# First graph-attention layer: masks straight from the transposes, two sets of mask tiles, a part of chunk 0 made in the loop

## The chip, the cores and the metric

The kernel runs on one core of a Trainium2 chip. The metric is the device time of one execution in microseconds (us); lower is better. The core has TensorE (PE), VectorE (DVE), ScalarE (ACT) and GpSimd (POOL). SyncE (SP) computes nothing here; it issues most of the transfers, one after the other, from its own queue, and a transfer that has to wait holds up those behind it.

## The reference, cut to what matters

There are N = 4096 nodes with 256 features and an adjacency matrix of 4096 x 4096 int32. Layer 0 is a graph attention and an FFN of 30 steps; layer 1 has two graph attentions and a routed FFN of six experts. All three graph attentions use the same adjacency:

```
h  = einsum('nf,hfd->hnd', layernorm(x), W)         # 4 heads of 64
f1 = h . a1 ; f2 = h . a2                           # per node and head
e  = leaky_relu(f1[:, :, None] + f2[:, None, :], 0.2)
e  = where(adj > 0, e, -9e15)
out = elu(softmax(e) @ h)
```

## The kernel before, in words

**The attention without an exponential per pair.** exp of a leaky ReLU is one of two products, exp(f1)exp(f2) or its version with slope 0.2; which one is told by the sign of f1 + f2. So per node j the preparation writes two scaled copies of h (tile `vals`, in two f16 parts), and the loop only makes, for every pair, a byte that says which copy counts: `st` where the sign says "above" and the edge exists, `below` where the edge exists and the sign says otherwise. PE multiplies `vals` by these byte tiles (FP8, 0x38 is 1.0).

**The order.** `attention` is called for g0 (layer 0), g1 and g2 (layer 1). Each call has a preparation over 8 groups of 512 nodes (`columns`, `products`, `upper`, `lower`; L259 to L383) and then a loop over 128 units: 4 chunks of 1024 target nodes, 4 heads, 8 blocks q of 4 x 128 source nodes. In the loop a unit has
- four steps (`step_of`, L445): `st` <- sign(f1 + f2), on ACT (L459), or for the fourth step of some units on DVE (L457: two units of five in chunks 0 to 2 of g0, else four of five). Steps are written one unit ahead (LEAD = 1); the tile `st` has 4 buffers.
- two DVE instructions, L585 (`st` and mask) and L591 (mask xor `st`, into `below`, 3 buffers).
- 64 matmuls of the unit before (L535).
- at times an instruction of the closing of the head before (L466 to L497, L631, L632).

**The masks.** A mask tile `m` holds one group g of 1024 source nodes for one chunk: 1 MB as bytes, made of four pieces. A piece starts as 256 rows x 1024 columns of adj (1 MB int32, `rows_a`, 3 buffers, loaded at L203), is turned to bytes by one DVE instruction (L211, `rows_p`) and transposed by a DMA (L217). In g0 the 16 pieces of chunk 0 are made in the preparation, two after each group (`first_masks`, L222), straight into the four buffers of `m`, and each full tile is stored to `edges` in DRAM (L230). The pieces of chunk c + 1 are made in the loop of chunk c, by a generator (`make`, L502) that takes one unit for load, conversion and transpose into the tile `turned`, and the next unit for the store of these 256 KB to `edges` (L513). From chunk 1 on the loop reads its masks back from `edges` (`load_mask`, L191, called at L600). Layers g1 and g2 load every mask from `edges`.

**What sets the order.** Tile pools are opened and closed as a stack: a pool opened after the preparation's pools are closed lies in the memory these had, and the first instruction that writes there waits for the last one that used it. The pool `work` of the loop (L439), with `st` and `below`, is such a pool, and so is `end` (closings) in g0; in g1 and g2 `end` is opened before the preparation (L182). DVE and ACT run the loop in the written order (`manual_schedule`, L553). Everything else is ordered by a planner with its own estimates of costs: it may put an instruction that is ready ahead of one that stands earlier in the code, in the loop's surroundings too.

**Rows.** x and later rows come through the pool `stream` (4 buffers of 512 KB, L61, loaded at L96 on SP). At the end of g0's loop the first groups of x1d, the layer's result, are asked for (L607); the FFN takes these four groups at L705, measures them (L682, L684), and computes their rates on ACT and POOL (L690 to L694), for which it needs the constants `eps` (L661, POOL).

Of the kernel before, what the change touches and what calls it, by code (L numbers as in the profile page):

```python
# [11 lines left out]
F32 = mybir.dt.float32  # L12
# [34 lines left out]
def gnn_ffn_kernel(ctx: ExitStack, tc: tile.TileContext, a: dict, out: bass.AP):  # L47
# [13 lines left out]
    stream = ctx.enter_context(tc.tile_pool(name="stream", bufs=4))  # L61
# [26 lines left out]
    ahead = {}  # L88


    def rows_in():
        return stream.tile([P, G * C], F32, name="rows")

    def load_ahead(src, g, view=rows_of):
        t = rows_in().rearrange("p (r c) -> p r c", c=C)
        nc.sync.dma_start(t, view(src, g))  # L96
        ahead[g] = t
# [67 lines left out]
    def attention(tag, src, norm, w, others, chunks, first, ends, following):  # L165
# [7 lines left out]
        with ExitStack() as scope:  # L173
# [5 lines left out]
            mask = scope.enter_context(tc.tile_pool(name=f"{tag}_mask", bufs=4))  # L179
            fpool = scope.enter_context(tc.tile_pool(name=f"{tag}_f", bufs=2))  # L180

            end = None if first else scope.enter_context(tc.tile_pool(name=f"{tag}_end", bufs=1))  # L182
            masks, f1b = {}, {}
# [7 lines left out]
            def load_mask(c, g):  # L191

                m = masks[c, g] = mask.tile([P, 4, 8, TR], F8, name="m")
                nc.sync.dma_start(m, edges[c, g])

            arow, prow = {}, {}

            def load_piece(c, n):

                g, part = n // 4, n % 4  # L200
                i0 = c * CM * P + part * TR
                arow[n] = pieces.tile([P, 2, 8 * P], I32, name="rows_a", bufs=3)
                nc.sync.dma_start(  # L203
                    arow[n],
                    adj[i0 : i0 + TR, g * 8 * P : (g + 1) * 8 * P].rearrange("(p s) n -> p s n", s=2),
                )

            def to_bytes(n):

                prow[n] = pieces.tile([P, 8 * P, 2], I8, name="rows_p", bufs=2)  # L210
                nc.vector.tensor_scalar(  # L211
                    prow[n].rearrange("p n s -> p s n"), arow.pop(n), 0, ONE8, op0=OP.is_gt, op1=OP.mult
                )

            def turn(dst, n):

                nc.sync.dma_start_transpose(  # L217
                    dst.rearrange("p j n -> p (j n)").bitcast(BF16).rearrange("p (j n) -> p j n", j=8),
                    prow.pop(n).rearrange("p n s -> p (n s)").bitcast(BF16),
                )  # L220

            def first_masks(n):  # L222

                g, part = n // 4, n % 4
                if part == 0:
                    masks[0, g] = mask.tile([P, 4, 8, TR], F8, name="m")
                to_bytes(n)
                turn(masks[0, g][:, part], n)
                if part == 3:
                    nc.sync.dma_start(edges[0, g], masks[0, g])  # L230

            with ExitStack() as ps:
# [19 lines left out]
                def load(g):  # L252
                    if g in ahead:
                        rows[g] = ahead.pop(g)
                    else:
                        load_ahead(src, g)
                        rows[g] = ahead.pop(g)
# [126 lines left out]

                if first:
                    load_piece(0, 0)
                load(0)
                load(1)
                if first:
                    for n in (1, 2):  # L390
                        load_piece(0, n)
                if not first:
                    load_mask(0, 0)
                late = [functools.partial(make, prep, small_ps, get(prep)) for get, make in others]
                for g in range(NG + 2):
# [14 lines left out]
                    if first:  # L410
                        for n in range(2 * g, min(2 * g + 2, 16)):
                            first_masks(n)
                            if n + 3 < 16:
                                load_piece(0, n + 3)
# [21 lines left out]

            if first:
                end = scope.enter_context(tc.tile_pool(name=f"{tag}_end", bufs=1))
# [4 lines left out]
            steps, accs = {}, {}  # L443

            def step_of(at, s):  # L445
# [5 lines left out]
                if s == 0:  # L451
                    steps[at] = work.tile([P, 4, JU, TR], I8, name="st", bufs=4)
# [47 lines left out]
            todo = []  # L500

            def make(c):  # L502

                load_piece(c, 0)
                load_piece(c, 1)
                for n in range(16):
                    if n + 2 < 16:
                        load_piece(c, n + 2)
                    to_bytes(n)
                    t = pieces.tile([P, 8, TR], F8, name="turned", bufs=3)  # L510
                    turn(t, n)
                    yield
                    nc.sync.dma_start(edges[c, n // 4, :, n % 4], t)  # L513
                    yield

# [34 lines left out]
            closing, making = None, None  # L552
            with tc.manual_schedule(engines={mybir.EngineType.DVE, mybir.EngineType.Activation}):  # L553
# [3 lines left out]
                for at in range(len(units) + LAG):  # L557
# [5 lines left out]
                    if at < len(units):  # L563
                        c, h, q = units[at]
                        if q == 0 and h == 0 and first and c + 1 < len(chunks):
                            making = make(c + 1)
# [26 lines left out]
                    if b >= 0:  # L593
# [5 lines left out]
                        if bh == H - 1 and bq % 2 == 1 and bc + 1 < len(chunks):  # L599
# [3 lines left out]
                    if making is not None:  # L603
                        next(making, None)
                    if at == len(units) - (4 if first else 2):
                        for g in range(3 if first else 2):
# [37 lines left out]
    attention("g0", x, True, w0, [make, *makers], [8, 8, 8, 8], True, to_rows(x1d, x), [x1d])  # L644
# [9 lines left out]
    with ExitStack() as scope:  # L654
# [16 lines left out]
        def load(g):  # L671
            if g not in ahead:
                load_ahead(x1d, g)
# [31 lines left out]
        for g in range(4):  # L705
            load(g)
# [652 lines left out]
```

## Time and profile before

| what | us |
|---|---|
| time, median of 3 runs (3040.38 to 3043.03) | 3040.51 |
| the profiled execution: its time | 3040.38 |
| its span on the profile | 3038.7 |
| PE / DVE / ACT / POOL busy, of the span | 2810.8 / 2713.6 / 2423.7 / 1160.5 |
| g0: first L585 of the loop; L585 of unit 96 (first of chunk 3) | 108.76; 488.32 |
| end of g0's loop on DVE (last L591) | 605.2 |
| g1: first L585 of the loop | 1663.24 |
| g2: first L585 of the loop | 2206.39 |

How to read it: the windows view gives the busy time of each engine in a stretch, with the number of instructions in brackets. A timeline line gives start and duration in us, engine, line of the code, operation, output <- input tiles, shape and count; what stands in square brackets is the idle time of the engine just before and what ended it. Instructions of one engine overlap a little, so the distance from start to start is a few hundredths of a us shorter than the duration. "SPq" is SP's queue. "st<-f1b,nf" and "vals<-v" name tiles without their buffer numbers.

### The profile page before, as it was taken

What the parts mean: (1) busy time and instruction counts of PE and PEld (TensorE: products, weight loads), DVE (VectorE), ACT (ScalarE), POOL (GpSimd) and SP (SyncE); (2) the same over time, 40 slices, a digit from 0 to 9 for tenths busy, and PEclk for the clock granted to TensorE, in tenths of its full rate; (3) what the DMA queues carried; (4) which work ended last, traced back from release to release, by engine and by line L of the source; (5) the groups of instructions that cost most, each with busy time, mean ns of one, the idle gap of its engine ahead of it and who ended that gap; (6) DMA issues with size and microseconds to landing.
All of it is one profiled execution on the core that took longest, in us unless ns stands there. A gap on an engine that the chain in (4) does not pass through costs nothing. (4 is left out here: it accounts for less than half of the span.)

```text
span 3038.7 us, 80983 instructions
## 1 busy us (share of the span) xinstructions
PE 2810.8 (93%) x33327; PEld 2549.8 (84%) x33327; DVE 2713.6 (89%) x5529; ACT 2423.7 (80%) x3011; POOL 1160.5 (38%) x1052
## 2 busy tenths in 40 slices
PE   6799999969999999999998999999899999975994
PEld 5699999958888888888876999999699999964883
DVE  8799999989999999999997899999789999975445
ACT  4799999888888888888866999999699999951220
POOL 2000000079999999999992000000300000022762
PEclk9899999979999999999998999999999999987997
DMA  9989995143333333333343032120302232141225
GB/s 307 275 246 291 270 266 147 29 132 67 70 67 67 70 67 69 69 67 70 67 98 113 20 102 71 55 85 20 110 23 92 66 95 87 37 146 56 96 93 200
DMA packets 491339, 332.55 MB, mean 109 GB/s; under 512 B 417342, under 2 KB 446171, under 8 KB 484827
## 3 DMA queue, kind: packets, MB, share of 16 engines
q1 hardware_dynamic: 476722, 301.81, 37.3%
q0 software_dynamic: 7104, 19.41, 2.0%
q10 hardware_dynamic: 7144, 6.16, 0.7%
q8 instruction: 263, 4.31, 0.6%
q14 instruction: 106, 0.86, 0.1%
HBM read 195.58 MB, written 52.04 MB: 81 GB/s over the span
## 5 line engine op out<-in xcount | busy, mean ns | idle before, releaser
L535 PE MATMUL acc<-vals,st 128*128 128x130 f16 x12288 | 1431.9, 219 | 59.8 <-DVE st L585 32.0
L535 PE MATMUL acc<-vals,below 128*128 128x130 f16 x12288 | 1431.3, 221 | 2.2 <-DVE below L591 2.2
L459 ACT ACTIVATE st<-f1b,nf 128x1024 int8<-128x1024 f32 x1265 | 1331.0, 1141 | 10.0 <-DMA fd<-rt 6.1
L535 PEld LDWEIGHTS <-st 128*128 128x128 fp8e4 x12288 | 1208.8, 98 | 33.4 <-issue 33.4
L535 PEld LDWEIGHTS <-below 128*128 128x128 fp8e4 x12288 | 1177.5, 96 | 36.4 <-issue 33.4
L869 PE MATMUL po<-wT,zT 128*128 128x256 f32 x1920 | 576.1, 382 | 7.1 <-ACT zT L852 7.1
L872 PE MATMUL po<-w,zT 128*128 128x256 f16 x3840 | 577.9, 273 | 0.4 <-DMA zT<-z 0.4
L833 POOL TENSOR_TENSOR th<-th,y 128x1024 f32<-128x1024 f32 x240 | 567.4, 2364 | 27.3 <-ACT th L832 5.0
L872 PEld LDWEIGHTS <-zT 128*128 128x128 f16 x3840 | 376.3, 98 | 161.9 <-DMA zT<-z 1.5
L591 DVE TENSOR_TENSOR below<-m,st 128x1024 int32<-128x1024 int32 x384 | 470.0, 1224 | 32.7 <-DVE st L585 0.9
L585 DVE TENSOR_TENSOR st<-st,m 128x1024 int32<-128x1024 int32 x384 | 467.7, 1218 | 13.7 <-ACT st L459 13.7
L809 DVE SCALAR_TENSOR_TENSOR y<-po,z_rs,bias 128x256 f32<-128x256 f32 x928 | 384.4, 477 | 2.0 <-PE tp L802 0.7
L845 DVE BATCH_NORM_STATS2 z_st<-z 128x6 f32<-128x256 f32 x960 | 335.7, 413 | 0.0
L869 PEld LDWEIGHTS po<-wT,zT 128*128 128x128 f32 x1920 | 291.1, 192 | 17.1 <-ACT zT L852 8.7
L821 ACT ACTIVATE z<-th 128x1024 f32<-128x1024 f32 x240 | 251.1, 1046 | 8.6 <-POOL th L833 8.3
L832 ACT ACTIVATE th<-y 128x1024 f32<-128x1024 f32 x240 | 249.9, 1041 | 0.1
L856 POOL TENSOR_TENSOR z_rs<-z_rs,mhalf 128x4 f32<-128x4 f32 x240 | 244.7, 1019 | 0.0
L852 ACT COPY zT<-tp 128x512 f32<-128x512 f32 x240 | 140.2, 584 | 110.4 <-PE tp L802 110.3
L457 DVE TENSOR_SCALAR st<-f1b,nf 128x1024 int8<-128x1024 f32 x271 | 201.2, 743 | 5.4 <-DMA fd<-rt 2.7
L661 POOL MEMSET eps<- 128x1 f32 x1 | 0.1, 98 | 520.1 <-DVE u L487 520.1
L1028 POOL IOTA along_i<- 128x37 int32 (+1 forms) x2 | 2.4, 1212 | 501.5 <-DMA ew<-in_L_ffn_expert_w_dram 501.5
L435 POOL MEMSET hs<- 128x4 f32 x3 | 0.3, 101 | 495.0 <-DVE u L487 495.0
(233 smaller groups left out, 3021.5 us busy)
## 6 DMA issues: line engine op xcount, KB each, us to landing
rows_a<-in_adj_dram SPq DMA_DIRECT2D x64, 1024.0 KB
m<-edges SPq DMA_DIRECT2D x44, 1024.0 KB
f1b<-fd SPq DMA_DIRECT2D x48, 512.0 KB
edges<-turned SPq DMA_DIRECT2D x48, 256.0 KB
y<-yd SPq DMA_DIRECT2D x16, 512.0 KB
rows<-x1d SPq DMA_DIRECT2D x12, 512.0 KB
ew<-in_L_ffn_expert_w_dram SPq DMA_DIRECT2D x18, 256.0 KB
rows<-in_x_dram SPq DMA_DIRECT2D x8, 512.0 KB
```

The costliest lines, as they stand in the source:

```text
L459: nc.scalar.activation(out, f1, AF.Sign, bias=f2, scale=-1.0)
L535: nc.tensor.matmul(acc[:, i, cols], masked[part][:, at_i // TR, s, rows], v[:, cols], start=(j == 0 and part == 0), stop=(j == NT - 1 and ...
L585: nc.vector.tensor_tensor(above, above, whole, OP.bitwise_and)
L591: nc.vector.tensor_tensor(below, whole, above, OP.bitwise_xor)
L809: nc.vector.scalar_tensor_tensor(y[:, g * G + r, :], po[:, r, :], rstd[:, r : r + 1], last if end else bias, op0=OP.mult, op1=OP.add,)
L821: nc.scalar.activation(z, th.pop(u), AF.Silu, scale=0.01)
L832: nc.scalar.activation(th[at], y[:, g * G : (g + 1) * G, :], AF.Tanh, scale=0.01)
L833: ins = nc.gpsimd.tensor_tensor(th[at], th[at], y[:, g * G : (g + 1) * G, :], OP.add)
L845: nc.vector.bn_stats(st[:, r, :], z[:, r, :])
L856: nc.gpsimd.tensor_tensor(rs[u], rs[u], mhalf, OP.pow)
L869: nc.tensor.matmul(po[:, r, :], src[:, r * P : (r + 1) * P], wT, start=True, stop=False)
L872: nc.tensor.matmul(po[:, r, :], src16[:, part * G + r, :], w16[:, other, :], start=False, stop=(part == 1 and other == 1),)
```

## The change

The change does these things:
- In g0 a second set of four mask tiles (`mask1`) is opened after the preparation. Chunks 0 and 2 use the first set, chunks 1 and 3 the second. Every transpose writes straight into a mask tile; `turned`, the stores of 256 KB and the reload of chunks 1 to 3 are gone. A full tile is stored once, 1 MB, two pieces after it is full.
- 12 of the 16 pieces of chunk 0 are made in the preparation (1 or 2 after each group). Pieces 12 to 15 are made in the units 0 to 3 of the loop, the 16 of chunk 1 in the units 4 to 31; later chunks have one piece in two units.
- The int32 piece `adj` has 2 buffers instead of 3, in a pool that is closed after g0 and whose place `stream` then takes. The load of piece n + 2 is issued after the conversion and transpose of piece n. In g0 the x rows come through a tile `t` of the preparation, 3 buffers, and the first group of x is issued ahead of the first piece.
- `st` gets a pool of its own, opened ahead of the preparation, in all three layers. `end` is opened after the preparation in all three.
- The FFN's first four loads of x1d are issued from POOL instead of from SP at the end of g0's loop.

```diff
-    stream = ctx.enter_context(tc.tile_pool(name="stream", bufs=4))
+    stream = []
-    def load_ahead(src, g, view=rows_of):
-        t = rows_in().rearrange("p (r c) -> p r c", c=C)
-        nc.sync.dma_start(t, view(src, g))
+    def load_ahead(src, g, view=rows_of, queue=nc.sync):
+        t = stream[-1].tile([P, G, C], F32, name="rows")
+        queue.dma_start(t, view(src, g))
...
-            mask = scope.enter_context(tc.tile_pool(name=f"{tag}_mask", bufs=4))
+            mask = [scope.enter_context(tc.tile_pool(name=f"{tag}_mask", bufs=4))]
-            end = None if first else scope.enter_context(tc.tile_pool(name=f"{tag}_end", bufs=1))
+            spool = scope.enter_context(tc.tile_pool(name=f"{tag}_steps", bufs=4))
...
+            PREP = 12
+            PER = 4 * (NT // 8)
+            def load_piece(n):
+                c, g, part = n // PER, n % PER // 4, n % 4
+                i0 = c * CM * P + part * TR
-                arow[n] = pieces.tile([P, 2, 8 * P], I32, name="rows_a", bufs=3)
+                arow[n] = stream[-1].tile([P, 2, 8 * P], I32, name="adj")
                 nc.sync.dma_start(arow[n], ...)
+            def make_piece(n):
+                if n >= len(chunks) * PER:
+                    return
+                c, g, part = n // PER, n % PER // 4, n % 4
+                if part == 0:
+                    masks[c, g] = mask[c % 2].tile([P, 4, 8, TR], F8, name="m")
+                pair = pieces.tile([P, 8 * P, 2], I8, name="pair")
+                nc.vector.tensor_scalar(pair..., arow.pop(n), 0, ONE8, op0=OP.is_gt, op1=OP.mult)
+                nc.sync.dma_start_transpose(masks[c, g][:, part]..., pair...)
+                if n + 2 < len(chunks) * PER:
+                    load_piece(n + 2)
+                if part == 1 and n > 4:
+                    store_mask(n // 4 - 1)
+            def store_mask(n):
+                c, g = n // (PER // 4), n % (PER // 4)
+                nc.sync.dma_start(edges[c, g], masks[c, g])
...
+                    elif first:
+                        rows[g] = work.tile([P, G, C], F32, name="t", bufs=3)
+                        nc.sync.dma_start(rows[g], rows_of(src, g))
...
+                load(0)
                 if first:
-                    load_piece(0, 0)
-                load(0)
+                    load_piece(0)
                 load(1)
                 if first:
-                    for n in (1, 2):
-                        load_piece(0, n)
+                    load_piece(1)
...
                     if first:
-                        for n in range(2 * g, min(2 * g + 2, 16)):
-                            first_masks(n)
-                            if n + 3 < 16:
-                                load_piece(0, n + 3)
+                        for n in range(PREP * g // 8, min(PREP * (g + 1) // 8, PREP)):
+                            make_piece(n)
...
+            end = scope.enter_context(tc.tile_pool(name=f"{tag}_end", bufs=1))
             if first:
-                end = scope.enter_context(tc.tile_pool(name=f"{tag}_end", bufs=1))
+                mask.append(scope.enter_context(tc.tile_pool(name=f"{tag}_mask1", bufs=4)))
...
-                    steps[at] = work.tile([P, 4, JU, TR], I8, name="st", bufs=4)
+                    steps[at] = spool.tile([P, 4, JU, TR], I8, name="st")
...
-                        if bh == H - 1 and bq % 2 == 1 and bc + 1 < len(chunks):
+                        if not first and bh == H - 1 and bq % 2 == 1 and bc + 1 < len(chunks):
                             load_mask(bc + 1, bq // 2)
...
-                    if making is not None:
-                        next(making, None)
-                    if at == len(units) - (4 if first else 2):
-                        for g in range(3 if first else 2):
+                    if first:
+                        u = at % (H * NJ)
+                        if at < H * NJ:
+                            due = PREP + u + 1 if u < PER - PREP else PER + (u - 3) * PER // 28
+                        else:
+                            due = PER * (at // (H * NJ) + 1) + (u + 1) // 2
+                        while made < due:
+                            make_piece(made)
+                            made += 1
+                        if at == len(units) - 30:
+                            store_mask(len(chunks) * PER // 4 - 1)
+                    if not first and at == len(units) - 2:
+                        for g in range(2):
                             load_ahead(*following[:1], g, *following[1:])
...
-    attention("g0", x, True, w0, [make, *makers], [8, 8, 8, 8], True, to_rows(x1d, x), [x1d])
+    with tc.tile_pool(name="adj", bufs=2) as adjacency:
+        stream.append(adjacency)
+        attention("g0", x, True, w0, [make, *makers], [8, 8, 8, 8], True, to_rows(x1d, x), [])
+    stream.append(ctx.enter_context(tc.tile_pool(name="stream", bufs=4)))
...
         for g in range(4):
-            load(g)
+            load(g, nc.gpsimd)
```

## The prediction

> **What bounds the kernel now.** I read the windows first, one for the preparation of layer g0 and one for each chunk of its loop.
>
> ```profile
> core 0: us, PE busy (x) PEld busy (x) DVE busy (x) ACT busy (x) POOL busy (x), PEclk, DMA share, GB/s
> 108.00:234.00 126.00, 117.42 (x1958) 116.70 (x1959) 117.06 (x119) 126.00 (x127) 0.00 (x0) 0.96 0.95 271
> 234.00:361.00 127.00, 122.48 (x2088) 121.98 (x2086) 122.66 (x130) 126.30 (x128) 0.00 (x0) 0.99 1.02 276
> 361.00:488.00 127.00, 121.15 (x2065) 120.65 (x2063) 123.22 (x131) 126.82 (x129) 0.00 (x0) 0.99 1.03 267
> 488.00:604.00 116.00, 113.31 (x1958) 112.82 (x1956) 110.13 (x124) 106.88 (x109) 0.00 (x0) 1.00 0.15 41
> ```
>
> ```profile
> 12.00:103.00 91.00, 65.16 (x275) 50.52 (x273) 81.38 (x169) 40.75 (x67) 25.14 (x40) 0.90 1.00 301
> ```
>
> In chunks 0 to 2 ScalarE (ACT) has no free time, VectorE (DVE) has 9, 4 and 4 us, and the DMA engines are busy throughout. In chunk 3, which makes no masks, TensorE (PE) is nearest to full. In the preparation DVE is the busiest engine (81 of 91 us); ACT is half idle. DVE's conversions (L211) waited for nothing there: the lines view gives their 64 instructions 0.1 us of idle time.
>
> Next, the timeline where the preparation meets the loop:
>
> ```profile
> 98.13 2.44 DVE L376 SCALAR_TENSOR_TENSOR vals<-vals,v 128x1040 f16<-128x1040 f16 x2
> 99.20 0.23 ACT L340 COPY rt<-sp 32x128 f32<-32x128 f32 x1
> 100.49 2.36 DVE L211 TENSOR_SCALAR rows_p<-rows_a 128x2048 int8<-128x2048 int32 x2
> 103.50 0.64 SPq L341 DMA_DIRECT2D fd<-rt  x1
> 105.50 7.39 ACT L459 ACTIVATE st<-f1b,nf 128x1024 int8<-128x1024 f32 x7 [6.07 <-DMA fd<-rt]
> 105.52 1.42 DVE L457 TENSOR_SCALAR st<-f1b,nf 128x1024 int8<-128x1024 f32 x2 [2.67 <-DMA fd<-rt]
> 108.76 1.23 DVE L585 TENSOR_TENSOR st<-st,m 128x1024 int32<-128x1024 int32 x1 [1.83 <-ACT st L459]
> 110.20 0.37 PE L535 MATMUL acc<-vals,st 128*128 128x130 f16 x2 [14.09 <-DVE st L585]
> ```
>
> The first step tiles (L459, L457) wait for a DMA that reads rt, a tile of the preparation. They need no data from it; they wait because they lie in memory that the preparation gives back. Then DVE waits for ACT's three steps, and PE starts 14 us after its last work. Layer g1 has the same joint (g2 too: last L376 over at 2203.1, first L585 at 2206.39):
>
> ```profile
> 1657.51 2.44 DVE L376 SCALAR_TENSOR_TENSOR vals<-vals,v 128x1040 f16<-128x1040 f16 x2
> 1659.98 12.58 ACT L459 ACTIVATE st<-f1b,nf 128x1024 int8<-128x1024 f32 x12 [1.31 <-DVE vals L376]
> 1663.24 1.22 DVE L585 TENSOR_TENSOR st<-st,m 128x1024 int32<-128x1024 int32 x1 [1.78 <-ACT st L459]
> ```
>
> From there g1 and g2 are bound by PE: in the windows 1800:1900 and 2300:2400 it is busy 99 of 100 us.
>
> **The change, part by part.** I sum against the profiled execution: 3040.38 us (span 3038.7 and 1.7 around it), 0.13 under the median of 3040.51.
>
> *Four conversions leave the preparation.* A conversion holds DVE 1.14 us from its start to the next start (L211 at 254.35, next at 255.46). Four are 4.6 us, at DVE's pace. If the chain through POOL's rstd and b held the end instead, only the two conversions queued after the last L376 count, 2.3. If the DMA held it: 301 GB/s over 91 us are 27.4 MB; two piece loads and a store fewer are 3 MB, 10 us. I take 4.6, since DVE is the fullest of the compute engines.
>
> *The steps get memory of their own (spool).* The wait for rt's DMA goes (2.67 us on DVE), and unit 0's steps can be made in ACT's idle time before, which takes away the 3.24 us from 105.52 to 108.76. What is late next is the end of DVE's preparation. That the planner moves loop work ahead is seen elsewhere: L905, written behind the FFN, issues at 140.36, and POOL runs the FFN loop's L833 at 623.41 before L752 of its preparation at 629.36. So 2.67 + 3.24 = 5.9, bounds 0 and 5.9. `below` still lies in given-back memory, but its L591 comes after the last L376 on DVE anyway. In g1 and g2 the same saves 1663.24 - 1659.95 = 3.3 and 3.2. If L585 itself also moves ahead, 1.3 more each; none if the steps stay behind.
>
> *x rows load ahead of the first piece.* DVE idles 10.06 us at the start, for the weights; the statistics of two groups (3.5 us) could fill that. I take 0, bounds 0 and 3.5.
>
> *Four more pieces in chunk 0's loop.* 4 x 1.14 = 4.6 us on DVE, beside ACT, which is full for 126 us while DVE has 9 free: nothing. Without that cover it is 4.6. But ACT may now start ahead by the other three step buffers (units 1 to 3: 11 steps; 19 took 19.86 us, so 1.045 each, 11.5 us), and then DVE is the bound. Its work for 96 units, from start to start: 96 x 2.45 (L585 and L591), 52 x 1.13, 38 x 0.66 (L457), 11 closings x 5.3, in all 377.4 against the 379.56 from L585 of unit 0 to that of unit 96 now: 2.2 us to gain. Against that: with two piece buffers the load of piece 14 issues after piece 12 is converted and its turn issued (1.3 + 0.6 us). The shortest issue-to-use now is 7.0 us (104.21 to 111.17, without a wait), so at most 8.9 where two units of 3.7 less a conversion leave 6.3. That is up to 2.6 us, twice at most (pieces 14 and 15). I take 1.2 for it, so a net gain of 1.0; bounds -5.2 and +2.2. PE behind needs 3.69 us a unit and stays under DVE.
>
> *No reload, one store for four.* Twelve 1 MB loads go and 48 stores of 256 KB become twelve of 1 MB. No compute engine waited for m<-edges, so 0. SP waited 99 us ahead of these stores, with pieces queued behind; the new store comes two pieces after its last turn. After the twelve go, a piece's load has less beside it; I price neither.
>
> *x1 loads on POOL.* Four loads leave SP (276 and 406 us) for POOL, which has nothing from 95.9 to 615.98, where it waits for memory to write eps. The tiles come free after the last conversion (482 us), DVE first reads them at 603.64. 0 if they stand ahead of the eps memsets; else the third rival.
>
> A rule of the Trainium skill speaks against this part. In that execution DVE is busy 110 of 116 us from 488 to 604. "SBUF — State Buffer", section "SBUF: two separate sides", says that a DMA issued from GpSimd has its descriptors written by GpSimd's cores, which are locked out while DVE runs a two-port fast mode, and advises the other queues. No row here shows a POOL load beside this loop. By the rule each load could stretch into DVE's gaps; with some 120 us before the use that is still 0.
>
> Sum: 4.6 + 5.9 + 1.0 + 3.3 + 3.2 = 18.0; 3040.4 - 18.0 = **3022**. Extremes: 10 + 5.9 + 3.5 + 2.2 + 4.6 + 4.5 = 31 saved (3009); 2.3 - 5.2 saved where no step moves ahead (3043).
>
> **Rivals.**
> 1. *The gaps hide it.* From 80 us on DVE's preparation has six gaps of about 1 us that wait for POOL or PE; conversions sit between them. If the chain sets the end and steps stay behind the preparation's ACT work: 2.3 + 2.67, and 1.3 in g1 and g2 each (the wait on L376): 7.6, **3033**. For it: the last two groups (L364 to L364) take 13.1 and 11.6 us where the eight take 9.2 on average; against: DVE is 89% full over the whole.
> 2. *Slower: steps in the way.* Steps put early stand on ACT in front of hc (L316) and bd (L323), which the preparation's chain waits for. Four units are 14 ACT steps a layer, 42 in three, 43.9 us. If each delays the chain by its length, 3022 + 43.9 = 3066; 17 of 42 eat the gain, and from 24 the kernel is over 0.2% slower. For it: in g2's preparation ACT is nearly full from 2184 to 2198. Against: a step put into a gap costs the chain only what overhangs. For 30 of 42: **3053**.
> 3. *The x1 loads stand behind eps.* Issued at 616.1, with 1 us for the issue and 2.7 to land (a gather at 2784.97), statistics 1.7 after that: rate starts near 621.5 instead of 616.3, 5.2 later, of which 1.7 is covered because z (632.3) waits for scale till 633.9. +3.5: **3026**. Against: POOL sits idle, and on SP these loads already ran 200 us ahead.
> 4. *The pieces come late.* Two buffers for three: it doesn't do what it says if DVE, which never waits for a piece now, starts to. Three such waits of 2.6 us, in the preparation or in units 2 to 5: 7.8, **3030**.
>
> **How the numbers follow.** Forecast 0.50 (own range 3012 to 3032), rivals 0.17, 0.12, 0.10, 0.11. The range 3007 to 3040 leaves out most of rival 2 and the tails. About 0.2% (6 us) is what a measurement tells from no change: faster than 3034.4 holds the forecast, rivals 3 and 4 and 0.13 of rival 1, that is 0.84; within, 0.04 of rival 1 and 0.04 of rival 2, 0.08; slower, the rest of rival 2, 0.08.
>
> **What would show it.** Right: first L585 of g0 near 98 us without a wait for DMA fd<-rt; first L585 of g1 and g2 at the end of the last L376; L459 in ACT's idle time of the preparation; ACT no longer full in chunk 1; DVE waits for adj below 3 us in units 2 to 5; x1 loads landed by 590. Wrong: a distance of over 6.68 us between the L364 pairs of g1, DVE waits for adj, or DVE x_st waiting for rows at the FFN's start.

## The result, and the profile after

The kernel after takes 3024.49 us (median of 6 runs, 3022.3 to 3026.32) where the kernel before takes 3040.45 (6 runs, 3037.28 to 3043.03): a ratio of 0.9947, with a 95% interval of 0.9934 to 0.996, 16 us less. Its profiled execution took 3026.16 us, with a span of 3024.4 (before: 3038.7).

Line numbers have moved. In the kernel after, the `and` of a unit is L567 (L585 before) and its xor, which makes `below`, L573. ACT's steps are L461, DVE's L459, the conversions L214, the last DVE work of the preparation L380, PE's products L519. First the windows of the kernel after, the preparation of g0 and then its four chunks:

```profile
core 0: us, PE busy (x) PEld busy (x) DVE busy (x) ACT busy (x) POOL busy (x), PEclk, DMA share, GB/s
12.00:94.00 82.00, 60.88 (x267) 47.26 (x267) 76.20 (x159) 54.21 (x81) 25.61 (x41) 0.96 1.02 296
94.00:223.00 129.00, 120.68 (x1977) 119.13 (x1978) 121.59 (x124) 115.54 (x116) 0.00 (x0) 0.94 0.95 260
223.00:350.00 127.00, 121.92 (x2089) 120.45 (x2087) 122.67 (x130) 126.50 (x129) 0.00 (x0) 1.00 0.86 238
350.00:477.00 127.00, 120.76 (x2069) 119.28 (x2067) 123.49 (x132) 126.30 (x130) 0.51 (x1) 1.00 0.81 227
477.00:594.00 117.00, 113.61 (x1936) 113.15 (x1934) 109.59 (x123) 106.11 (x107) 3.26 (x4) 0.99 0.19 55
```

The preparation is 9 us shorter, and ACT is fuller in it (54 of 82 us instead of 41 of 91): steps of the loop run there. Chunk 0 takes 129 us instead of 126. Chunks 1 and 2 take what they took, with ACT full as before, though the DMA share fell from about 1.02 to 0.86 and 0.81.

Then the timeline of the kernel after, at the joints where preparations meet loops (g0 first, then g1):

```profile
88.65 0.64 SPq L345 DMA_DIRECT2D fd<-rt  x1
...
91.80 2.38 DVE L380 SCALAR_TENSOR_TENSOR vals<-vals,v 128x1040 f16<-128x1040 f16 x2
...
94.11 1.21 DVE L567 TENSOR_TENSOR st<-st,m 128x1024 int32<-128x1024 int32 x1
...
95.37 0.40 PE L519 MATMUL acc<-vals,st 128*128 128x130 f16 x2 [7.10 <-DVE st L567]
...
1647.68 2.44 DVE L380 SCALAR_TENSOR_TENSOR vals<-vals,v 128x1040 f16<-128x1040 f16 x2
...
1650.21 1.23 DVE L573 TENSOR_TENSOR below<-m,st 128x1024 int32<-128x1024 int32 x1
```

The first `and` of g0 follows DVE's last L380 at once. The last score store is issued at 88.65, not at 103.50. In g1 the first `and` has gone into the preparation (1623.44), and the first xor follows the last L380.

To see where the time went I cut the spans of six kernels at the same marks. Unit 32 is the first of chunk 1; "po" is the FFN's first product into that tile. e1 to e9 are experiments told below.

| start, us | g0's last `and` | FFN's first po | g1's unit 32 | g2's unit 32 | g2's last `and` | span |
|---|---|---|---|---|---|---|
| before | 602.50 | 640.94 | 1782.29 | 2325.87 | 2680.46 | 3038.7 |
| after | 592.50 | 630.90 | 1768.11 | 2318.14 | 2672.77 | 3024.4 |
| e1 | 589.45 | 627.85 | 1765.01 | 2307.23 | 2661.84 | 3021.2 |
| e2 | 588.68 | 627.08 | 1766.71 | 2307.63 | 2662.27 | 3013.7 |
| e3 | 595.62 | 643.49 | 1784.98 | 2338.03 | 2692.30 | 3051.4 |
| e9 | 589.57 | 627.95 | 1768.44 | 2321.14 | 2675.79 | 3035.5 |

From before to after, g0 gains 10.0 (14.65 at its start, less 3.1 in chunks 0 to 2 and 1.6 in chunk 3). The start of g1 gains 4.1. From g1 to g2 the kernel **loses** 6.5. From g2's last `and` to the end it gains 6.6. The last two nobody had forecast. g0's end has a spread of its own: e2's instructions on DVE and ACT stand in the order of the kernel after up to g1's preparation, and yet it ends 3.8 us sooner there. Chunk 3 is part of that spread: e1, e2 and e9 run it in 114.2 us, as the kernel before did, and after in 115.8 with the same instructions, at a granted PE clock of 0.99 instead of 1.00 and with PE busy 112.4 us instead of 110.8 (e2). So differences of 1 to 4 us in g0 between two single profiles are not read as effects here unless a wait shows them or several kernels agree.

### The profile page after: what moved, and what is told of

The parts are those of the page before. It is cut to its first block, busy times and chain, and to the rows that moved or that the text cites. A ratio compares the mean times of both kernels' runs of the same rounds, so it can differ in the third digit from the quotient of the medians.

```text
span 3024.4 us, 80903 instructions
## 1 busy us (share of the span) xinstructions
PE 2812.5 (93%) x33327; PEld 2549.3 (84%) x33327; DVE 2709.9 (90%) x5529; ACT 2422.3 (80%) x3011; POOL 1167.0 (39%) x1056
## 5 line engine op out<-in xcount | busy, mean ns | idle before, releaser
L519 PE MATMUL acc<-vals,st 128*128 128x130 f16 x12288 | 1433.7, 219 | 35.7 <-DVE u L472 27.5
L519 PE MATMUL acc<-vals,below 128*128 128x130 f16 x12288 | 1433.3, 221 | 12.3 <-DVE below L573 11.7
L461 ACT ACTIVATE st<-f1b,nf 128x1024 int8<-128x1024 f32 x1265 | 1334.3, 1142 | 32.1 <-PE acc L519 22.7
L519 PEld LDWEIGHTS <-below 128*128 128x128 fp8e4 x12288 | 1177.1, 96 | 48.7 <-issue 44.1
L519 PEld LDWEIGHTS <-st 128*128 128x128 fp8e4 x12288 | 1208.8, 98 | 9.5 <-DVE st L567 7.5
L573 DVE TENSOR_TENSOR below<-m,st 128x1024 int32<-128x1024 int32 x384 | 469.9, 1224 | 32.7 <-DVE st L567 1.2
L567 DVE TENSOR_TENSOR st<-st,m 128x1024 int32<-128x1024 int32 x384 | 466.9, 1216 | 1.1 <-ACT st L461 0.9
L105 POOL TENSOR_TENSOR ln_rstd<-ln_rstd,mhalf 128x4 f32<-128x4 f32 x24 | 32.0, 1334 | 562.0 <-ACT acc L998 491.8
L459 DVE TENSOR_SCALAR st<-f1b,nf 128x1024 int8<-128x1024 f32 x271 | 200.9, 742 | 6.8 <-PE acc L519 6.8
L818 DVE SCALAR_TENSOR_TENSOR z<-z,scale,z 128x512 f16<-128x512 f32 x240 | 179.0, 746 | 4.9 <-ACT z L817 4.9
```

The source lines that it names most:

```text
L461: nc.scalar.activation(out, f1, AF.Sign, bias=f2, scale=-1.0)
L519: nc.tensor.matmul(acc[:, i, cols], masked[part][:, at_i // TR, s, rows], v[:, cols], start=(j == 0 and part == 0), stop=(j == NT - 1 and ...
L567: nc.vector.tensor_tensor(above, above, whole, OP.bitwise_and)
L573: nc.vector.tensor_tensor(below, whole, above, OP.bitwise_xor)
```

## The experiments

**Theory:** the gain lies at the joints between stages. A tile that lies on memory which the stage before still uses must wait for it; the change moved such tiles. **Rivals:** the gain comes from the DMA traffic that went (reloads, small stores), or from the four conversions alone. Each kernel ran beside the kernel before in one session on one chip. Sessions differ: the kernel before took 3042 us beside e1 to e4 and e13, 3051 beside e5 to e9, 3056 beside e10 to e12. So ratios are compared; 0.001 is 3 us. Other moves of the change, such as the places of `adj` and `mask1`, no run takes back alone.

### The place of `end`: e1 and e2

The change also moved the pool `end` of g1 and g2 (with `e`, the last tile to be stored) behind the preparation. e1 opens it ahead again in both, e2 in g1 alone:

```
+            end = scope.enter_context(tc.tile_pool(name=f"{tag}_end", bufs=1)) if not first else None   # e2: if tag == "g1"
             spool = scope.enter_context(tc.tile_pool(name=f"{tag}_steps", bufs=4))
...
-            end = scope.enter_context(tc.tile_pool(name=f"{tag}_end", bufs=1))
+            end = end or scope.enter_context(tc.tile_pool(name=f"{tag}_end", bufs=1))
```

> The kernel after, with the pool `end` of g1 and g2 opened ahead of their preparation again, as it was before the change. Theory (which tiles a stage's first tiles lie on decides when it may start): g2's first x columns no longer lie on g1's last `e`, so ACT's wait of 5.28 us for the store of h1d goes and the start of g2 comes some 7.2 us sooner against g1's end; but the first tiles of the MoE's preparation lie on g2's last `e` again, and the 8.9 us that this joint gained are lost (1.9 of them were given back later in the MoE). Sum 3024.5 - 7.2 + 7.0 to 8.9 = 3024 to 3026, with PE idle between g2's last product and the MoE's first transpose at 15 to 16 us instead of 8.65. Rival (the place of `end` doesn't matter, both joints moved for another reason, the smaller DMA traffic or the steps' own memory): 3024.5 with both joints as they are in the kernel after, wait for h1d included.

> The kernel after, with `end` of g1 alone opened ahead of the preparation again; g2's stays behind it. Theory (place of tiles): the gain of the joint g2 to MoE stays, the loss of the joint g1 to g2 goes: 3024.5 - 7.2 = 3017 (3016 to 3020), no wait of ACT for the store of h1d at the start of g2. Rival (place doesn't matter): 3024.5. A third way: the wait goes, but PE's transposes or the x rows are late next at that joint, and 2 us or less come of it: 3022.5 to 3024.5.

Measured: e1 3024.14 us, ratio 0.9946 (0.9929 to 0.9962). e2 **3014.65 us**, ratio 0.9917 (0.9899 to 0.9934), the fastest kernel of this study. The two joints in the timeline are ACT's first xT of g2 (xT are the transposed rows, the first thing that a preparation writes on ACT) and DVE's first statistics of the MoE (the routed FFN behind g2). Before:

```profile
2149.03 0.60 ACT L270 ACTIVATE xT<-tp 128x512 f32<-128x512 f32 x1 [1.92 <-PE tp L117]
...
2699.76 1.40 DVE L104 BATCH_NORM_STATS2 ln_st<-rows 128x6 f32<-128x256 f32 x4 [3.56 <-DMA x3d<-e]
```

After:

```profile
2142.81 0.60 ACT L274 ACTIVATE xT<-tp 128x512 f32<-128x512 f32 x1 [5.28 <-DMA h1d<-e]
...
2682.07 0.75 DVE L100 BATCH_NORM_STATS2 ln_st<-rows 128x6 f32<-128x256 f32 x2 [0.45 <-PE acc L519]
```

e1:

```profile
2131.75 0.60 ACT L275 ACTIVATE xT<-tp 128x512 f32<-128x512 f32 x1 [1.92 <-PE tp L113]
...
2682.30 1.41 DVE L100 BATCH_NORM_STATS2 ln_st<-rows 128x6 f32<-128x256 f32 x4 [4.38 <-DMA x3d<-e]
```

e2:

```profile
2133.49 0.60 ACT L275 ACTIVATE xT<-tp 128x512 f32<-128x512 f32 x1 [1.92 <-PE tp L113]
...
2671.56 0.75 DVE L100 BATCH_NORM_STATS2 ln_st<-rows 128x6 f32<-128x256 f32 x2 [0.45 <-PE acc L520]
```

The brackets tell it; e1's total alone fits the theory and the rival alike. With `end` ahead in g1, g2's xT waits for PE's transposes and not for the last store of g1; with it behind, xT waits for that store (h1d<-e). At the MoE it is the other way round: with `end` of g2 ahead, the statistics wait for g2's last store (x3d<-e), with it behind they don't. None of these waits is for data: where the wait is absent, xT and the statistics run before the last store has even been issued (e2: 2137.36 and 2679.14). In the table, e1's stretch from g1's to g2's unit 32 is 7.8 us shorter than after (542.2 against 550.0) and its stretch from g2's last `and` to the end 7.8 longer (359.4 against 351.6). e2 has the good end of both. Its 10 us of gain hold 9.1 from the stretch from g1 to g2; the 3.8 that its g0 ended sooner are spread, and 2.4 of them were given back by g1's unit 32. The theory stands; e2 even came out a little under its 3016 to 3020.

### The steps' own memory: e3 and e9

e3 puts `st` back into `work` in all three layers:

```
-            spool = scope.enter_context(tc.tile_pool(name=f"{tag}_steps", bufs=4))
...
-                    steps[at] = spool.tile([P, 4, JU, TR], I8, name="st")
+                    steps[at] = work.tile([P, 4, JU, TR], I8, name="st", bufs=4)
```

e9 does so in g1 and g2 alone and keeps the pool as a reservation in its place, so that the tiles of the preparation lie as after:

```
             spool = scope.enter_context(tc.tile_pool(name=f"{tag}_steps", bufs=4))
+            if not first:
+                hold = spool.tile([P, 4, 4, JU, TR], I8, name="hold", bufs=1)
+                nc.gpsimd.memset(hold[:, 0, 0, 0, :4], 0)
...
-                    steps[at] = spool.tile([P, 4, JU, TR], I8, name="st")
+                    steps[at] = (spool if first else work).tile([P, 4, JU, TR], I8, name="st", bufs=4)
```

> The kernel after without the steps' own pool: `st` lies in `work`, which opens after the preparation, as before the change; all the rest of the change stays. Theory (memory of the steps lets them move into the preparation): g0's first `and` goes from 94.1 back to about 100 (2.67 of wait and 3.24 of steps), g1's joint loses 4.4, g2's joint loses 4.5 and gets back the 3.5 by which its preparation had grown: 3024.5 + 5.9 + 4.4 + 1.0 = 3035.8 (3033 to 3038). Rival (the gain comes from the four conversions and from the DMA traffic that went, 12 reloads and 48 small stores): the steps are worth 3 us or less, 3024 to 3027.5.

> The kernel after; in g1 and g2 the steps' own pool is kept as a reservation of the same size in the same place (a tile of it that nobody uses), while the steps lie in `work` behind the preparation, as before the change. So the tiles of the preparation and of `end` lie as in the kernel after, and the steps can't move ahead. Theory: g1's start loses the 4.4 us that its joint gained, g2's start loses 4.5 and gets back 3.5 of preparation (first to last L368 back from 42.9 to 39.5): 3024.5 + 5.4 = 3030 (3028 to 3032); ACT's wait for the store of h1d at g2's start stays, since the place of `end` is what makes it. Rival (placement alone made these joints, the steps' moving ahead brings nothing): 3024.5 and joints as after. Rival 2 (in g2 the moved steps cost more than they bring): g2's start sooner by 1 us or more than after, 3027 or less.

Measured: e3 3054.06 us, ratio 1.0045 (1.0028 to 1.0061), slower than the kernel before and 18 us past the theory's figure. e9 3039.44, ratio 0.9962 (0.995 to 0.9975). Timeline of e3 at the start of g0's loop and of the FFN:

```profile
95.93 1.42 DVE L458 TENSOR_SCALAR st<-f1b,nf 128x1024 int8<-128x1024 f32 x2 [2.50 <-DMA fd<-rt]
99.16 1.23 DVE L566 TENSOR_TENSOR st<-st,m 128x1024 int32<-128x1024 int32 x1 [1.81 <-ACT st L460]
...
617.88 0.50 ACTq L702 DMA_DIRECT2D ln<-in_L_ffn_ln_w_dram  x1
```

The old wait for fd<-rt is back, and the first xor comes at 100.42 instead of 95.65: 4.8 us for g0. By the table, e3 loses against after 3.1 to g0's end, 4.3 at g1's start and 3.0 from g1 to g2. These 10.4 lie where the steps are, near the 11.3 that the theory had. But also 9.5 from g0's end to the FFN's first product and 7.5 in the MoE, together 17. With the pool gone the later tiles lie elsewhere, and at the MoE the wait shows it: DVE's statistics there wait 3.73 us for x3d<-e again, g2's xT waits 5.38 for h1d<-e as in the kernel after, and the FFN's weights load 16 us later than after (ln at 617.88; after: 601.85), behind two groups of x1's rows on ACT. That these 9.5 us at the FFN also come from the place of tiles is argued, not shown: ACT's queue shows no wait there, only another order.

In e9 the timeline of DVE at g1's joint reads:

```profile
1643.57 2.44 DVE L383 SCALAR_TENSOR_TENSOR vals<-vals,v 128x1040 f16<-128x1040 f16 x2
1646.10 1.42 DVE L462 TENSOR_SCALAR st<-f1b,nf 128x1024 int8<-128x1024 f32 x2
1649.30 1.22 DVE L570 TENSOR_TENSOR st<-st,m 128x1024 int32<-128x1024 int32 x1 [1.78 <-ACT st L464]
```

From the end of the last L383 to the first xor (1650.56) are 4.5 us; after: 0.1. Against that, the eight groups of the preparation go faster without the steps: from the first to the last pair of L368 (DVE's two products per group; L371 in e9) g1's takes 47.6 instead of 49.3, g2's 39.5 instead of 42.9. Net, from first xT to first xor, the steps bring 3.3 us in g1 (69.65 in e9 against 66.35) and 2.0 in g2 (59.40 against 57.36). xT still waits 5.29 us for h1d<-e, as it should. The mechanism is right; the sum in these two layers is 5.3 for 5.4 expected, less in g1 and more in g2. e9's total holds more than these joints: its MoE statistics start 3.1 us after g2's last `and` (after: 9.3), and the stretch behind it is 2.9 us shorter than in e7 of the same session. The cause of that stays open.

### Pieces in the preparation: e4, e11, e12, e13

e4, e12 and e13 change one number, `PREP = 12`, to 16, 14 and 10 (e13 with e2's edit). e11 is e4 with g0's score stores issued by ACT:

```
-                    nc.sync.dma_start(
+                    (nc.scalar if first else nc.sync).dma_start(
                         fd[:, g * GR : (g + 1) * GR].rearrange("s (t p) -> t s p", p=P), rt
```

> The kernel after with all 16 pieces of chunk 0 made in the preparation again (two per group), none of them in chunk 0's loop; the pieces of chunk 1 follow the same rule as after. Theory: the four conversions in the preparation cost between 4.6 (what the prediction had) and 8.7 (the 14.65 that the start of g0 gained less the steps' 5.9), and chunk 0 gets back the 3.4 by which it had grown: 3024.5 + 1.2 to 5.3 = 3025.7 to 3029.8. Rival (a conversion costs in the loop what it costs in the preparation, so that it doesn't matter where it is made): 3024.5, start later and chunk 0 shorter by the same amount.

> The kernel with all 16 pieces of chunk 0 in the preparation, and in g0 the stores of the scores to `fd` issued by ACT, which makes them, instead of SP. In the kernel with 16 pieces the first `below` came at 118.0 and not at about 103, after 9.15 us of waiting for the store fd<-rt, which SP issued only at 110.9, behind the transposes of pieces whose rows had come late. Theory (SP's order is what made the four pieces cost 22 us): the store goes right after its copy at about 97, the first `below` comes at 109 or sooner (after the last conversion), chunk 1 starts at 235 instead of 244.3: 9 us less than with 16 pieces, 3037 where the kernel before takes 3040.4. Rival (the two adjacency buffers are the cause and the store only the last of several things that were late): first `below` still at 115 to 118, 3043 to 3046.

> The kernel after with 14 instead of 12 pieces in the preparation. Theory (SP's order: each piece more puts a transpose and a load ahead of the last score store): the step between 12 (first `below` 95.7) and 16 pieces (118.0) is not due to DVE's four conversions of 1.23 us, and 14 pieces lie well above DVE's share: first `below` at 101 to 107, a total of 3029 to 3034 where the kernel before takes 3040.4. Rival (DVE's work alone counts up to a point, and only the last two pieces are caught in the queue): first `below` at 98, given back in chunk 0, 3024.5 to 3026.

> The kernel with `end` of g1 alone opened ahead of its preparation (3015 where the kernel before takes 3041, ratio 0.9917), with 10 instead of 12 pieces in the preparation and six in the first units of chunk 0. With 16, 14 and 12 pieces the first `below` came at 118.0, 107.1 and 95.7; with 16 and the score stores on ACT's queue at 103.4. Theory (below 12 no store waits for SP any more, so a piece less is worth what it was with the stores on ACT, 7.7 us over four, 1.9 each, at the start, and 0.86 each are given back in chunk 0): first `below` at 91.5 to 93, chunk 0 longer by 1.7, the total 2 us less: 3013, ratio 0.9905 to 0.9917. Rival (pieces 14 and 15 are made in units 4 and 5 and needed in unit 6; DVE has 3.97 us per unit and the six conversions take 7.4 of the first 24 us): a stall of 3 to 8 us in units 4 to 7, 3016 to 3021, ratio 0.992 to 0.9936. If the straight line went on (5.6 us a piece), the first `below` would come at 84.5.

Measured:

| pieces in the preparation | first xor of g0 | first xor to that of unit 32 | ratio, 95% interval |
|---|---|---|---|
| 16 (e4) | 118.03 | 127.6 | 1.0019 (1.0009 to 1.0029) |
| 16, stores on ACT (e11) | 103.36 | 127.6 | 0.9975 (0.9964 to 0.9986) |
| 14 (e12) | 107.14 | 126.8 | 0.9985 (0.9976 to 0.9994) |
| 12 (after) | 95.65 | 128.8 | 0.9947 (0.9934 to 0.996) |
| 10 (e13; beside e2: 0.9917) | 94.70 | 139.4 | 0.995 (0.9937 to 0.9964) |

e4 missed both expectations: 22 us for four pieces, where DVE's part is 4.9. The timeline of e4 shows the chain:

```profile
107.65 1.23 DVE L214 TENSOR_SCALAR pair<-adj 128x2048 int8<-128x2048 int32 x1 [3.58 <-DMA adj<-in_adj_dram]
...
108.91 1.25 SPq L217 DMA_TRANSPOSE m<-pair  x1
...
110.89 0.74 SPq L345 DMA_DIRECT2D fd<-rt  x1
...
118.03 1.23 DVE L573 TENSOR_TENSOR below<-m,st 128x1024 int32<-128x1024 int32 x1 [9.15 <-DMA fd<-rt]
```

The last piece's rows come late (two buffers), so its conversion is late. Its transpose waits at the head of SP's queue, and behind it stands the last score store, whose rt was done at 96.5 (ACT's copy, L344, at 96.25). The first `below` waits for that store, since it lies on rt's memory. Of the 9.15 us, 2.0 pass before the store is issued and 7.1 between its issue and the end of the wait. In e11 the store leaves from ACT at 93.82, right after its copy (93.54), and the wait is gone:

```profile
102.22 1.23 DVE L214 TENSOR_SCALAR pair<-adj 128x2048 int8<-128x2048 int32 x1 [0.73 <-DMA adj<-in_adj_dram]
103.36 1.22 DVE L573 TENSOR_TENSOR below<-m,st 128x1024 int32<-128x1024 int32 x1
```

The start comes 14.7 us sooner than in e4, against 9 expected, and g0's last `and` too (597.14 against 611.76). The store's place in SP's queue was two thirds of the 22 us; the four pieces without it are 103.36 - 95.65 = 7.7, of which DVE's conversions are 4.9 (its waits for adj in the preparation also grew, from 0.8 to 4.5). With 14 pieces the same wait, before the first `below`, still stands at 9.2 us: rt was copied at 87.52, the store issued at 98.74, behind two transposes. The total of e12 lies 11.6 us over after by ratio, more than either expectation. With 10 pieces both expectations were missed. The start gains 1.0 only, because the last score store is still what ends last there: issued at 87.25, it is waited for at 94.70. And pieces made in the loop are late, as the rival had it, but by more than its 3 to 8 us: DVE waits 4.4 us for adj in units 2 to 5 and 6.3 for a transposed piece in unit 6, chunk 0 takes 11.4 us more than e2's, and the ratio of 0.995 is over the rival's 0.9936. Timeline of e13, the start and unit 6:

```profile
94.70 1.23 DVE L574 TENSOR_TENSOR below<-m,st 128x1024 int32<-128x1024 int32 x1 [0.21 <-DMA fd<-rt]
...
127.26 1.23 DVE L568 TENSOR_TENSOR st<-st,m 128x1024 int32<-128x1024 int32 x1 [6.33 <-DMA m<-pair]
```

So twelve is best of the four.

### What chunk 0 costs: e5 and e10

e5 takes DVE's steps in chunk 0 from two in five units to one:

```
-                if s == JU - 1 and at % 5 < (2 if first and c + 1 < len(chunks) else 4):
+                if s == JU - 1 and at % 5 < ((1 if c == 0 else 2) if first and c + 1 < len(chunks) else 4):
```

> The kernel after, with one step in 20 of chunk 0 on DVE instead of two in 20 (6 or 7 steps of 0.75 us move to ACT, at 1.05 us each); all else stays. Theory (chunk 0 grew by 3.44 us because DVE, with the four pieces more, has no real slack there, while ACT works 115.5 of 129 us): DVE's work in chunk 0 falls by 4.8, ACT's grows by 6.7 to 122, and chunk 0 takes 2 to 3.4 us less: 3021 to 3022.5. Rival (late pieces, so the DMA at a share of 0.95 in chunk 0): chunk 0 stays at 129, 3024.5. If ACT is the bound after all: chunk 0 longer by 2 or more, 3026.5.

(Its "one step in 20" counts the four steps of each of five units.) Measured: ratio 0.9964 (0.995 to 0.9978). Chunk 0 did not get shorter. From xor to xor it takes 128.7 us (after: 128.8); from `and` to `and` 131.7 (after: 129.0), but e5's first `and` runs ahead of the last work of the preparation, 1.6 us sooner than after's, while its first xor comes 1.2 later, so that the second pair of marks overstates it. The theory is refuted; between the rival (129, late pieces) and the third way (ACT is the bound) the run does not decide. The same late piece stands in both kernels, in after as

```profile
106.26 1.23 DVE L214 TENSOR_SCALAR pair<-adj 128x2048 int8<-128x2048 int32 x1 [2.33 <-DMA adj<-in_adj_dram]
```

and in e5 with 2.34 us. ACT's restart in the kernel after, then windows of e5 and of the kernel after from there on:

```profile
102.93 5.31 ACT L461 ACTIVATE st<-f1b,nf 128x1024 int8<-128x1024 f32 x5 [10.52 <-PE acc L519]
```

```profile
103.00:224.00 121.00, 115.39 (x1960) 114.47 (x1958) 110.50 (x111) 119.55 (x120) 0.00 (x0) 0.99 0.93 260
```

```profile
103.00:223.00 120.00, 114.26 (x1913) 112.95 (x1910) 112.99 (x116) 115.47 (x116) 0.00 (x0) 0.97 0.96 261
```

ACT's idle 13.5 us in chunk 0 lie mostly at its start: 10.5 us in one wait for PE with all four step buffers full. From 103 on it has 4.5 us left, and in e5 1.5. So ACT's 13 us are not room for more steps. DVE's free 9 us were of another kind: before, 6.2 of its 9.5 idle us in chunk 0 were waits for ACT's steps (L459). In the kernel after these are 0.9; that is what the head start brought, and the four conversions and the late piece took it.

e10 (with e2's edit) makes the last four pieces of every chunk in that chunk's first units, so that chunk 0 makes 16 and not 20:

```
-                        if at < H * NJ:
-                            due = PREP + u + 1 if u < PER - PREP else PER + (u - 3) * PER // 28
-                        else:
-                            due = PER * (at // (H * NJ) + 1) + (u + 1) // 2
+                        due = PER * (at // (H * NJ)) + (PREP + u + 1 if u < PER - PREP else PER + (u - 3) * PREP // 28)
...
-                        if at == len(units) - 30:
+                        if at == len(units) - 24:
```

> The kernel with `end` of g1 alone opened ahead of its preparation, and in it the last four pieces of every chunk, not of chunk 0 alone, made in the first four units of their own chunk: chunks 0, 1 and 2 make 16 pieces each (chunk 0 made 20) and chunk 3 makes 4 (it made none). Theory (chunk 0 grew by 3.4 us since DVE and the restarted ACT have no slack there; chunk 3 is bound by PE and has some): chunk 0 takes 125.5 to 127 instead of 128.2, chunks 1 and 2 as before, chunk 3 at most 1.5 more than its 114.2; at the time of the kernel with `end` moved (3015 where the kernel before takes 3041), 1 to 3 us less: 3012 to 3014, a ratio of 0.9908 to 0.9915 instead of 0.9917. Rival (four conversions cost the same in any chunk): no change, 3015, chunk 3 longer by what chunk 0 is shorter.

Measured: ratio 0.9972 (0.9963 to 0.9981), 17 us worse than e2. Chunk 0 takes 125.5 us as forecast, but chunks 1, 2 and 3 take 135.6, 131.3 and 124.2: four pieces in four units at a chunk's start are late each time (in chunk 1 DVE waits twice for adj, 4.8 us). So the four pieces were chunk 0's 3.4 us (the late one stays, 2.8 us of waiting), and moving that load to the later chunks costs more than it frees. Neither expectation had that.

### Traffic and the queue of x1: e8 and e7

e8 reads each stored mask tile of chunks 1 to 3 back into itself; e7 lets SP issue the first x1 loads:

```
                 nc.sync.dma_start(edges[c, g], masks[c, g])
+                if c > 0:                                          # e8
+                    nc.sync.dma_start(masks[c, g], edges[c, g])    # e8
...
-            load(g, nc.gpsimd)
+            load(g)                                                # e7
```

> The kernel after, with each stored mask tile of chunks 1 to 3 read back into its own tile right after its store (12 loads of 1 MB, the bytes that the change took away; the data are the same). Theory (the DMA traffic that went was hidden): 3024.5 to 3026, the loop's unit 0 to 96 within 1 us of 382.6. Rival (the reload was part of the cost, DMA shares of 0.81 to 0.95 in the loop leave no room): 12.6 MB more at the 230 to 260 GB/s of the loop are 50 us of DMA time in 383, and pieces come late: 3 us or more, 3027.5 and over.

> The kernel after, with the first four loads of x1 issued by SP, as before the change, instead of POOL. Both queues must wait for the adjacency's memory until 476.5. Theory: on SP too they come more than 100 us ahead of the first statistics of x1 at 597.9, and a wait in SP's queue holds up no piece any more, since the last conversion is what they wait for: 3024.5, within 2. Rival (the loads stand in SP's queue ahead of pieces, stores or head rows that are due): chunk 2 or 3 of the first layer loses 2 to 5 us, 3026.5 to 3029.5.

Measured: e8 0.9956 (0.9939 to 0.9972). The DMA share rises to 1.02, 0.95 and 0.95 in chunks 0 to 2; chunks 1 and 2 take 1.3 and 0.9 more, g0's last `and` is 1.9 later, g2's 1.4; DVE waits 2.9 us for adj in these two chunks, where after has no such wait. Nearly all of the 12.6 MB is hidden, and the ratio is 0.0006 over that of e7, of the same session; the rival that the reloads made the gain falls. The 48 small stores were not put back. But they stood in chunks 0 to 2, and these took no less without them. e7 0.995 (0.9933 to 0.9966), g2's last `and` at 2672.18 against 2672.77: nothing, as expected.

## Why the prediction was right, and where it was not

The total was right (16 us for 18 forecast), by terms that were off and largely made up for each other. In the spans, g0's start brought 14.4 for 10.5 forecast, chunks 0 to 2 lost 3.1 for a gain of 1.0, chunk 3 lost 1.6, which is spread, and everything behind g0 brought 4.3 for 6.5. So coming within 2 us is partly luck.

- *Four conversions leave the preparation: 4.6, bounds 2.3 to 10.* Too small, though inside the bounds. From before to e3, which has all but the steps' memory, the first xor comes 9.6 us sooner (110.02 to 100.42), 1.4 of it at the first L364 already, by the earlier x rows; four pieces put back without SP's order cost 7.7 (e11), with it 22 (e4). The step costed each piece as DVE work alone. But the last wait at this joint is for the last score store, 2.67 us in before and 2.50 in e3. Its rt is copied at 99.20 and 86.92, SP issues it at 103.50 (behind a transpose at 101.75) and 88.43, and it is waited for until 105.5 and 95.9. That the store came so much sooner than four conversions explain has not been taken apart: DVE's idle time in the preparation fell too, by 2.7 us between its first L364 and its last `vals`.
- *The steps get memory of their own: 5.9, 3.3, 3.2.* Mechanism right, sizes 4.8 in g0 (e3) and 3.3 and 2.0 in g1 and g2 (e9). The xor stays out of the preparation and the first `and` goes into it. Rival 2, steps in the way, is true on a small scale: 1.7 us in g1's preparation and 3.4 in g2's, far from the 18 that would eat the gain. (Its 14 ACT steps a layer hold for g0; in g1 and g2 DVE makes the fourth step of all four units, so 38 in three layers, not 42.)
- *x rows ahead of the first piece: 0 to 3.5.* The first statistics come at 5.34 instead of 13.96 us, the first L368 at 29.94 instead of 31.14 (its L364); 1.2 here, 1.4 in e3.
- *Four more pieces in chunk 0: a gain of 1.0, bounds -5.2 and +2.2.* The sign was wrong: chunks 0 to 2 take 3.1 longer (0.7 to 3.2 in after, e1, e2, e7 and e9, which share g0's code), and it lies in chunk 0 (2.6 to 3.6). "DVE has 9 free" was read from a sum. The work from start to start that the step added up (377.4) was compared with 379.56 as if ACT's lead could fill the rest of all three chunks. The lead did take DVE's waits for steps out of chunk 0 (6.2 to 0.9 us), but four step buffers end it there (10.5 us of waiting on ACT), and chunks 1 and 2 take what they took. Late pieces, rival 4, cost 2.3 us once, near twice the 1.2 that the step took.
- *No reload: 0.* Right within 2 us (e8).
- *x1 loads on POOL: 0.* Right: four issues took 3.77 us at 476.49, and the first statistics of x1, at 593.64, waited for nothing; on SP it is the same (e7). Rival 3 did not come: the loads stood ahead of the eps memsets (606.09). The Trainium skill ("SBUF — State Buffer", section "SBUF: two separate sides") warns of DMAs issued from GpSimd while DVE runs a two-port fast mode; with DVE busy 109.6 of 117 us no such delay can be seen in these four issues. Whether DVE was in that mode no run here shows.
- *Missing: the joints behind g0.* The diff moved `end` in g1 and g2 too, and the prediction gave that line no step. It lost 6.5 us from g1 to g2 and gained 6.6 in the MoE. That these two cancel is luck; e2, which keeps only the gain, shows it.

Of the signs that were named, ACT stays full in chunk 1 (126.5 of 127), which refutes a lead that lasts; the first `and` of g0 at 94.11 came even sooner than 98; DVE's one wait for adj in units 2 to 5 is under 3 us. A sign of being wrong, over 6.68 us between the pairs of g1, came too: four distances are over it (8.16, 7.28, 7.98 and 7.41), where before two were (9.73 and 7.28). But the eight groups take what they took (49.3 and 49.4).

## What to carry to other kernels

When a diff moves a pool, list for each stage behind it which first tiles lie on the tiles that the stage before stores last: here one pool's place decided 8 us at each of two joints, and opening it early in one stage and late in the next gave another 10. Cost a piece of work by all its instructions in every queue and by what stands behind them, not by its engine time alone. Before a free share of an engine is spent, look where it lies: ten idle us in one wait for buffers are not room in the loop.

## What the runs showed of the hardware

- A store of 16 KB that was ready at 96.5 us was issued at 110.9, because SP works its queue in order and a transpose ahead of it waited for a conversion (e4). From ACT's queue it needed no such wait (e11). The issue is not the landing: what waited for this store went on 7.1 us after its issue in e4 and 8.4 in e12 (98.74 to 107.14), and 2.0 in the kernel before (103.50 to 105.50).
- The place of tiles costs time without any change of instructions: e1, e2 and after have the same work, and 8 us lie between them at each of two joints. e3 and after lie 27 us apart, 17 of them in stretches without a step; a wait shows the cause for the MoE's 7.5 of these, not for the FFN's 9.5.
- Two sessions differ in one stage. e7's marks agree with after's within 0.6 us up to g2's last `and`; from there to the end it takes 362.6 us instead of 351.6, and the kernel before was 11 us slower beside it too. Whether the chip or the time makes this is open: the sessions with 3042 us (e1 to e4) and with 3051 us carry the same chip number.
